# Graph kernel, two layers on one Trainium2 core: half of the middle passes' pick one-hots built on the chip, node rows stored side by side, slot one-hots compared in pairs, overflow tiles shared by sixteen ranges

## The chip, the cores and the metric

The kernel runs on one core of one Trainium2 chip. The metric is the device time of one execution, in microseconds (us). The core has TensorE (PE; its weight loads are shown apart as PEld), VectorE (DVE), ScalarE (ACT), GpSimd (POOL) and SyncE (SP), each with a queue of its own, and 16 DMA engines that all queues share.

## The reference, cut to what matters

There are 32768 nodes with 128 features each and 524288 edges `src -> dst`. Layer 0 sums over edges, adds attention inside blocks of 512 nodes and a feed-forward part; layer 1 runs three passes, each of which sums over the edges in the other direction and adds a lookup in a table of 512 keys.

```python
agg = segment_sum(x[src], dst, num_segments=N)              # layer 0, once
h = relu(((1 + eps) * x + agg) @ W_loc1 + b_loc1) @ W_loc2 + b_loc2
...
for _ in range(3):                                           # layer 1
    retrieved = softmax((x @ Wq.T + bq) @ keys.T) @ values
    agg = zeros_like(x).at[row].add((dinv[:, None] * x)[col])
    lap = x - dinv[:, None] * agg
    x = 0.5 * x + 0.5 * (retrieved - 0.2 * lap)
return layernorm(x1 + layernorm(x))
```

So a sum over edges is needed four times: once in layer 0 (by `dst`) and three times in layer 1 (by `src`).

## The kernel before, in words

**Ranges and slots.** The nodes are cut into 256 ranges of 128. An edge belongs to a pair (own range, other range), and each pair has KS = 6 slots. A value is kept as three bf16 pieces, so a row is ROW = 384 bf16 elements (768 bytes; 772 in layer 0, which also counts edges). To move rows from one range to all others, a *pick* (a one-hot, 128 x 1536, fp8) is multiplied with the rows of a range: `spread` (L1406) makes 12 matmuls of 128x384 per range in six steps `m`, each step into one PSUM tile `exp` of two banks, which ACT casts to bf16 (L1416; every fourth step goes to DVE, in stage 5 every second), and stores two halves of 576 KB per range to `slots` in DRAM (L1419, SP's queue). The next pass fetches, for each range, 1152 KB of slots (`y_i`, L1424, SP's queue).

**What doesn't fit the slots.** Edges beyond six in a pair are listed: five tiles (OW) of 128 indices per range, gathered row by row by GpSimd's indirect DMA (L1429, `listed`), and, where five don't do, SH = 2 more tiles (`common`) that a group of GW = 8 ranges shares and that are gathered once a group. That is 5 + 2/8 = 5.25 gathers a range.

**Adding up.** `hot` (L1438) makes with one DVE instruction (L1440) the one-hots of all NC2 = 19 tiles of a range: 19 x 128 = 2432 elements a partition, comparing a ramp of 1 to 128 with the slot table, one value of which is read 128 times over (a step of 0). `add` (L1444) then makes 19 matmuls of 128x384 into the PSUM tile `seg`, the five listed tiles first. `Sums` (L1455) keeps fetches `lead` ranges ahead (6 in layer 0 and in the last pass, 2 in the middle) with lead + 1 buffers.

**Stages, in order.** (1) Attention, with the sorting of the edges woven in by a quota of DVE time (`edges`, L2120; `build` and `build_more` make the tables). (2) The spread of layer 0 (L1741), which makes its picks on the chip: three matmuls of 128x512 with a column of the identity (`listed_row`, L1385) copy the row of a range to all partitions, and DVE compares each with the partition's number (L1381). (3) The sums of layer 0 (L1802), with its own MLP and the picks of layer 1 (`keep_pick`), which are stored to DRAM, 192 KB a range. (4) The feed-forward part. (5) The first pass of layer 1 (L2035), spread and lookup only. (6) Two middle passes (L2063), in which the sums of block b + 2 are woven with the lookup and the spread of block b; `known_pick` (L1372) loads a pick for each range, two ahead (L1964). (7) The last pass (L2083), sums and two layer norms.

**What sets the order.** In stages 1, 3 and 7 the program's order is kept (`manual_schedule`). In the others the framework orders each engine's instructions by its own plan from the order of emission; in the middle passes the emission is `weave` (L1021) of some 41 steps of lookup and spread over 89 steps of sums per block. PSUM in the middle passes: two `seg` tiles (one bank each), two `exp` tiles (two banks each), one bank for `s`, one for `tr`.

**Rows in DRAM.** Node n = 512 b + 128 c + p lies in row n; a block's tile is [128 partitions p, 4 chunks c, D], so a transfer of a block (`rows_of`, L1316) moves 4 pieces per partition: 768 bytes each for `rows` (L1361), 512 bytes each for `part_d` and `x_d` (L1891, L1958, L1984, L1988).

Of the kernel before, what the change touches and what calls it, by code (L numbers as in the profile page):

```python
# [9 lines left out]
F32 = mybir.dt.float32  # L10
# [9 lines left out]
P = 128  # L20
# [11 lines left out]
OW = 5  # L32
GW = 8
SH = 2
# [375 lines left out]


class Grid:

# [129 lines left out]
    def build(self, pp):  # L543
# [9 lines left out]
        with tc.tile_pool(name="gr", bufs=1) as sp:  # L553
# [13 lines left out]
            for h in range(2):  # L567
                with tc.tile_pool(name=f"gr_h{h}", bufs=1) as hp:
# [89 lines left out]
                    with tc.tile_pool(name=f"gr_c{h}", bufs=1) as ap:  # L658
# [19 lines left out]
                        for t, n in ((0, 3), (3, OW - 3)):  # L678
# [7 lines left out]
                        yield two / 3  # L686
                        nc.vector.tensor_scalar(m, lw, main.oth, P - 1, op0=OP.logical_shift_right,
                                                op1=OP.bitwise_and)
                        yield two / 3
                        nc.vector.tensor_tensor(m, m, key, OP.bitwise_or)  # L690
                        yield one / 3
                        nc.vector.tensor_copy(fb[:, :OL], m)
# [116 lines left out]
    def build_more(self, lane, pp):  # L809
# [12 lines left out]
        with tc.tile_pool(name="mo", bufs=1) as sp:  # L822
# [10 lines left out]
            for h in range(2):  # L833
# [26 lines left out]
                yield L / 1000  # L860
                nc.vector.tensor_scalar(n, word, over.oth, P - 1, op0=OP.logical_shift_right, op1=OP.bitwise_and)
                yield L / 1000
                nc.vector.tensor_tensor(m, m, n, OP.bitwise_or)
                yield L / 1000
                nc.vector.tensor_tensor(val, m, valid, OP.mult)
                yield L / 1000
# [23 lines left out]
def tile_gnn_resnorm(ctx: ExitStack, tc: tile.TileContext, a: dict, out: bass.AP):  # L890
# [417 lines left out]
    def grid_consts(pool):  # L1308
        gc["iota1"] = pool.tile([P, P], BF16, name="iota1")
        nc.vector.tensor_scalar(gc["iota1"], iota, 1.0, None, op0=OP.add)  # L1310
        gc["lane1"] = pool.tile([P, 1], F32, name="lane1")
        nc.vector.tensor_scalar(gc["lane1"], lane_f, 1.0, None, op0=OP.add)
        gc["ident"] = pool.tile([P, P], BF16, name="ident_b")
        nc.vector.tensor_copy(gc["ident"], ident)

    def rows_of(t, i):  # L1316

        return t.rearrange("(b c p) d -> b p c d", c=NCH, p=P)[i]

    def ramp_in_psum(pool):  # L1320

        t = pool.tile([P, P], F32, name="ramp_p")
        nc.vector.tensor_copy(t, gc["iota1"])
        return t

    class Exchange:
# [12 lines left out]
        def load_rows(self, pool):  # L1339
            self.row = pool.tile([P, 2, SL], BF16, name="row")  # L1340
            nc.sync.dma_start(self.row.rearrange("p h f -> p (h f)"), self.grid["row"])

        def load_tables(self, pool):
            self.slot = pool.tile([P, NC2, NW], BF16, name="slot")
            nc.sync.dma_start(self.slot.rearrange("p c w -> p (c w)"), self.grid["slot"])
            self.other = pool.tile([P, NW, OW], I32, name="other")
            nc.scalar.dma_start(self.other.rearrange("p w c -> p (w c)"), self.grid["other"])
            self.shared = pool.tile([P, NW // GW, SH], I32, name="shared")
            nc.scalar.dma_start(self.shared.rearrange("p g c -> p (g c)"), self.grid["shared"])

        def split_steps(self, wp, b, x, rest):


            t = wp.tile([P, NCH, self.width], BF16, name="rows3")
            r = t[:, :, :ROW].rearrange("p c (o d) -> p c o d", o=3)
            if self.width > ROW:
                nc.gpsimd.memset(t[:, :, ROW:], 1.0)

            def end():
                nc.vector.tensor_sub(r[:, :, 2, :], rest, r[:, :, 1, :])  # L1360
                nc.sync.dma_start(rows_of(self.table, b), t)  # L1361
            return t[:, :, :ROW], [lambda: nc.scalar.copy(r[:, :, 0, :], x),
                                   lambda: nc.vector.tensor_sub(rest, x, r[:, :, 0, :]),
                                   lambda: nc.scalar.copy(r[:, :, 1, :], rest), end]
# [73 lines left out]
        def hot(self, wp, i, ramp, bufs):  # L1438
            oh = wp.tile([P, NC2, P], BF16, name="oh", bufs=bufs)
            nc.vector.tensor_tensor(oh, ramp[:, None, :].to_broadcast([P, NC2, P]),  # L1440
                                    self.slot[:, :, i].unsqueeze(2).to_broadcast([P, NC2, P]), OP.is_equal)
            return oh
# [414 lines left out]
    def layer1_grid(v_d, s3, c3):  # L1857

        exs = [Exchange("src", slots_d[t % 2], rows_d[t]) for t in range(T_STEPS)]
        with tc.tile_pool(name="l1g", bufs=1) as gp:  # L1860
# [9 lines left out]
            def first(b, st, wp, p_tr):  # L1870
# [18 lines left out]
                def norm():  # L1889
                    layer_norm(wp, st["x0"], st["x"])  # L1890
                    nc.sync.dma_start(rows_of(xs_d[0], b), st["x"])  # L1891
                return load, [(7, scale), (12, turn), (15, norm)]
# [26 lines left out]

            def emit(t, b, st, wp, p_e, p_s, p_tr, share):  # L1920

                ex = exs[t]
                y = {}

# [26 lines left out]
                def remain():  # L1951
# [5 lines left out]
                    nc.vector.scalar_tensor_tensor(part, st["x"], 0.4, part, op0=OP.mult, op1=OP.add)  # L1957
                    nc.sync.dma_start(rows_of(part_d, b), part)  # L1958
# [21 lines left out]
            def ask_part(t, b, wp):  # L1980

                if b < NB:
                    p_i = wp.tile([P, NCH, D], F32, name="part_i", bufs=3)
                    nc.scalar.dma_start(p_i, rows_of(part_d, b))  # L1984
                    parts[b] = [p_i]
                    if t == T_STEPS - 1:
                        x1 = wp.tile([P, NCH, D], F32, name="x1", bufs=3)
                        nc.scalar.dma_start(x1, rows_of(xs_d[0], b))  # L1988
                        parts[b].append(x1)
# [68 lines left out]
            with tc.tile_pool(name="l1w", bufs=2) as wp, \  # L2058
                    tc.tile_pool(name="l1_seg", bufs=2, space=PSUM) as p_g, \
                    tc.tile_pool(name="l1_exp", bufs=2, space=PSUM) as p_e, \  # L2060
                    tc.tile_pool(name="l1_s", bufs=1, space=PSUM) as p_s, \
                    tc.tile_pool(name="l1_tr", bufs=1, space=PSUM) as p_tr:
                for t in range(T_STEPS - 1):  # L2063
# [3 lines left out]
                    for w0 in range(2):  # L2067
                        ask_pick(wp, w0)
                    for n in range(-2, NB):
# [3 lines left out]
                        if n >= 0:  # L2073
                            lists.append(emit(t + 1, n, sts[n], wp, p_e, p_s, p_tr, 4))
                        two_b = placed(*lists)
# [102 lines left out]
```

## Time and profile before

| what | value |
|---|---|
| median of 3 runs (lowest, highest) | 14195.87 us (14195.01, 14202.4) |
| the profiled execution's own time | 14201.3 us |
| its span in the profile | 14199.4 us |
| mean granted TensorE clock | 0.927 |
| PE, DVE, ACT, POOL busy, share of the span | 86%, 80%, 47%, 43% |

| stage | from, to (us from the span's start) |
|---|---|
| 1 attention and sorting | 0 to 3530 |
| 2 spread of layer 0 | 3530 to 4531 |
| 3 sums of layer 0 | 4540 to 6232 |
| 4 feed-forward | 6250 to 6490 |
| 5 first pass of layer 1 | 6490 to 7965 |
| 6 two middle passes | 7965 to 12471 |
| 7 last pass | 12471 to 14199 |

The stages' bounds are the first and last start of their own instructions in the trace. A group's line gives the line of the kernel, the engine, the operation, what is written and read, how often, the busy time and the mean of one. DMA shares are the summed time of the packets over 16 engines; they can come out above 1. A line of waits names the waiting engine and line, who released it, the time in all, how often, and the longest.

### The profile page before, as it was taken

How to read it: one execution, taken by the hardware profiler on the slowest of the kernel's cores; microseconds unless marked ns; L12 is line 12 of the kernel's file. 1: busy time of each engine (PE TensorE's matmuls, PEld its weight loads, DVE VectorE, ACT ScalarE, POOL GpSimd, SP SyncE). 2: the span in 40 equal slices, each digit the busy share in tenths (PEclk: the TensorE clock that was granted, in tenths of full speed). 3: DMA queues.
4: the chain of work that ended last, by engine and by line, in shares of the span. 5: the costliest groups of instructions: out<-in, count | busy, mean ns of one | idle time of the engine just before them, and what ended most of it. 6: DMA issues, size and time to landing. Idle time of an engine off the chain costs nothing. (4 is left out here: it accounts for less than half of the span.)

```text
span 14199.4 us, 168166 instructions
## 1 busy us (share of the span) xinstructions
PE 12173.8 (86%) x58982; PEld 5828.9 (41%) x58982; DVE 11413.1 (80%) x16677; ACT 6658.1 (47%) x10316; POOL 6079.5 (43%) x5461
## 2 busy tenths in 40 slices
PE   8888888889887888888998799999899999966666
PEld 3232223333333444444444355555455555533333
DVE  7998998776998888877888677777677777778888
ACT  4343444334987111127888566666566666610000
POOL 0000000000001777740000477877688878767777
PEclk9898888888999999999999999999999999987787
DMA  1000000000999999977888899999999999988887
GB/s 40 11 11 17 10 11 12 18 8 33 348 346 348 309 309 309 310 242 261 304 311 308 299 383 385 390 383 383 350 376 386 382 391 381 383 292 285 286 283 256
DMA packets 1640075, 3602.99 MB, mean 254 GB/s; under 512 B 199346, under 2 KB 976466, under 8 KB 1638066
## 3 DMA queue, kind: packets, MB, share of 16 engines
q1 hardware_dynamic: 1165424, 2936.81, 55.6%
q0 software_dynamic: 258752, 533.02, 12.3%
q10 hardware_dynamic: 215042, 122.32, 2.8%
q8 instruction: 465, 7.62, 0.2%
q14 instruction: 392, 3.21, 0.1%
HBM read 2088.45 MB, written 1503.00 MB: 253 GB/s over the span
## 5 line engine op out<-in xcount | busy, mean ns | idle before, releaser
L1429 POOL DMA_INDIRECT listed<-rows,other x5120 | 5725.6, 1118 | 3544.2 <-issue 3151.1
L1416 ACT CAST y_o<-exp 128x768 bf16<-128x768 f32 x4224 | 3224.0, 808 | 1271.9 <-DMA slots<-y_o 627.2
L1411 PE MATMUL exp<-rows,pick 128*128 128x384 bf16 x12288 | 2768.2, 326 | 394.9 <-ACT y_o L1416 289.4
L1453 PEld LDWEIGHTS <-oh 128*128 128x128 bf16 x19456 | 1992.2, 102 | 2648.8 <-issue 1629.8
L1453 PE MATMUL seg<-y_i,oh 128*128 128x384 bf16 x12288 | 2745.0, 349 | 9.3 <-DMA y_i<-slots 9.3
L1416 DVE CAST y_o<-exp 128x768 bf16<-128x768 f32 x1920 | 1830.9, 954 | 687.4 <-PE exp L1411 636.2
L1411 PEld LDWEIGHTS <-pick 128*128 128x128 fp8e4 x12288 | 1185.1, 97 | 2115.5 <-issue 1550.7
L1453 PE MATMUL seg<-listed,oh 128*128 128x384 bf16 (+1 forms) x5120 | 1257.6, 336 | 815.5 <-DMA listed<-rows,other 777.2
L1606 ACT ACTIVATE pT<-s 128x1024 f32<-128x1024 f32 x1024 | 1021.5, 1023 | 1353.7 <-PE s L1602 1351.3
L1586 DVE TENSOR_REDUCE mx<-s 128x2 f32<-128x1024 f32 x1024 | 1204.4, 1219 | 270.5 <-PE s L1580 270.2
L1440 DVE TENSOR_TENSOR oh<-ramp_p,slot 128x2432 bf16<-128x2432 f32 x512 | 1372.3, 2681 | 12.7 <-DMA slot<-slot_dst 9.4
L1440 DVE TENSOR_TENSOR oh<-iota,slot 128x2432 bf16<-128x2432 bf16 x512 | 1373.7, 2683 | 3.0 <-DMA slots<-y_o 3.0
L283 POOL DMA_INDIRECT c_r<-pivots_over,c_ix x2 | 1.9, 946 | 3056.7 <-DVE c_ix L281 3056.4
L1602 PE MATMUL s<-ql,k 32*128 32x512 f32 x4096 | 1032.4, 692 | 259.2 <-DVE mx L1586 244.6
L2005 DVE SCALAR_TENSOR_TENSOR part_i<-seg,dinv,part_i 128x128 f32<-128x128 f32 x1536 | 529.6, 345 | 543.0 <-PE seg L1453 531.9
L1064 ACT ACTIVATE ln_rs<-ln_mv,eps_c 128x4 f32<-128x4 f32 x192 | 57.1, 297 | 1670.8 <-DVE ln_mv L1062 1489.7
L1930 PE MATMUL s<-keysT,qT 128*128 128x512 f32 x1536 | 818.2, 615 | 7.3 <-ACT pr L1043 3.7
L1453 PE MATMUL seg<-common,oh 128*128 128x384 bf16 (+1 forms) x2048 | 600.7, 350 | 194.5 <-DMA common<-rows,shared 194.2
L1942 PE MATMUL s<-pt,values 128*128 128x512 f32 x1536 | 750.6, 600 | 10.8 <-ACT pt L1937 10.6
L1580 PE MATMUL s<-k,q 32*128 32x512 f32 x4096 | 745.2, 726 | 6.0 <-DVE mx L1586 2.6
L1613 PE MATMUL pv<-pT,vx 128*32 128x512 f32 x4096 | 698.6, 751 | 0.2 <-ACT pT L1606 0.2
L1388 PE MATMUL row_p<-row,ident_b 128*128 128x512 bf16 x1536 | 601.8, 392 | 82.9 <-DVE pick L1381 62.3
(393 smaller groups left out, 14180.8 us busy)
## 6 DMA issues: line engine op xcount, KB each, us to landing
slots<-y_o SPq DMA_DIRECT2D x2048, 576.0 KB
y_i<-slots SPq DMA_DIRECT2D x1024, 1152.0 KB
pick<-pick SPq DMA_DIRECT2D x1024, 192.0 KB
listed<-rows,other POOLq DMA_INDIRECT x5120
rows<-rows SPq DMA_DIRECT2D x192, 384.0 KB
part_d<-part_o SPq DMA_DIRECT2D x192, 256.0 KB
part_i<-part_d ACTq DMA_DIRECT2D x192, 256.0 KB
rows<-rows SPq DMA_DIRECT2D x64, 386.0 KB
```

What stands on the lines that cost most here:

```text
L1411: nc.tensor.matmul(ps[:, j, :ROW], pick[:, o:o + P], r, start=True, stop=True)
L1416: (nc.vector.tensor_copy if to_dve else nc.scalar.copy)(dst, ps[:, :, :ROW])
L1429: nc.gpsimd.indirect_dma_start(out=g[:, k, :], out_offset=None, in_=self.table, in_offset=bass.IndirectOffsetOnAxis(ap=index[:, k:k + 1], ...
L1440: nc.vector.tensor_tensor(oh, ramp[:, None, :].to_broadcast([P, NC2, P]), self.slot[:, :, i].unsqueeze(2).to_broadcast([P, NC2, P]), OP.is ...
L1453: nc.tensor.matmul(ps[:, :n], oh[:, j, :], src, start=(k == 0), stop=(k == NC2 - 1))
L1580: nc.tensor.matmul(two[s // 2][:, s % 2, :], t["q", o][32 * s:32 * s + 32, c * P:(c + 1) * P], t["k", o][32 * s:32 * s + 32, :], start=Tru ...
L1586: nc.vector.tensor_reduce(m[:, c, 2 * i:2 * i + 2, xr[o]], st[b]["two"][i], AX.X, OP.max, negate=True)
L1602: nc.tensor.matmul(two[s // 2][:, s % 2, :], t["k", o][32 * s:32 * s + 32, c * P:(c + 1) * P], t["ql", o][32 * s:32 * s + 32, :], start=Tr ...
L1606: nc.scalar.activation(t["p", c][:, 2 * i:2 * i + 2, :], two[i], AF.Exp)
L1613: nc.tensor.matmul(t["o"][32 * s:32 * s + 32, :], t["v"][:, c, s, 2 * o:2 * o + 2, :].rearrange("p z e -> p (z e)"), t["p", c][:, s, :], s ...
L1930: nc.tensor.matmul(s, st["q"][:, c * P:(c + 1) * P], keysT, start=True, stop=True)
L1942: nc.tensor.matmul(ps, values[:, k, :], st["pt"][:, k, :], start=(k == 0), stop=(k == NCH - 1))
```

## The change

Four edits come together.

1. `GW` goes from 8 to 16: the two `common` tiles are shared by sixteen ranges, so 5.125 gathers a range.
2. Rows side by side: `kept_of` lays node (b, c, p) at row 512 b + 4 p + c, so that a block's transfer is one piece per partition (3072 bytes for `rows`, 2048 for `part_d` and `x_d`). The indices of the gathers have to name these rows: `row_index` makes them in `build` and `build_more`. The kernel's input and output stay as they were.
3. Pairs: the slot table is kept twice side by side, range first, so that the last dimension of every operand of `hot` is two bf16 elements next to each other; the two copies are made by DVE when the table is loaded (once in layer 0, once in layer 1). The ramp in PSUM (layer 0, last pass) becomes bf16, by a transpose on PE. In the middle passes the ramp is `iota1` in SBUF, as before.
4. In the middle passes every odd range's pick is made on the chip (`pick_steps`), during the spread of the even range before it: three matmuls of 128x512 into two `exp` tiles, ahead of the spread's steps 1 and 3, and two DVE comparisons of 1024 and 512 elements. Only the even ranges' picks are loaded. `row` (768 KB) is loaded once, ahead of the passes. In the first pass of layer 1 all picks are still loaded.

```diff
-GW = 8
+GW = 16
...
+def row_index(nc, dst, spare, window, lane):
+    n = NCH.bit_length() - 1
+    cost = dst.shape[-1] / 1000
+    lane(dst)
+    yield cost
+    nc.vector.tensor_scalar(dst, dst, n, None, op0=OP.logical_shift_left)
+    yield cost
+    nc.vector.tensor_scalar(spare, window, 7, NCH - 1, op0=OP.logical_shift_right, op1=OP.bitwise_and)
+    yield cost
+    nc.vector.tensor_tensor(dst, dst, spare, OP.bitwise_or)
+    yield cost
+    nc.vector.tensor_scalar(spare, window, 7 + n, 7 + n, op0=OP.logical_shift_right, op1=OP.logical_shift_left)
+    yield cost
+    nc.vector.tensor_tensor(dst, dst, spare, OP.bitwise_or)
+    yield cost
...
+        gc["down"] = pool.tile([P, P], BF16, name="down")
+        nc.vector.tensor_copy(gc["down"], gc["lane1"].to_broadcast([P, P]))
...
+    def kept_of(t, i):
+        return t.rearrange("(b p c) d -> b p (c d)", c=NCH, p=P)[i]
...
     def ramp_in_psum(pool):
-        t = pool.tile([P, P], F32, name="ramp_p")
-        nc.vector.tensor_copy(t, gc["iota1"])
+        t = pool.tile([P, P], BF16, name="ramp_p")
+        nc.tensor.transpose(t, gc["down"], gc["ident"])
         return t
...
         def load_tables(self, pool):
-            self.slot = pool.tile([P, NC2, NW], BF16, name="slot")
-            nc.sync.dma_start(self.slot.rearrange("p c w -> p (c w)"), self.grid["slot"])
+            self.slot = pool.tile([P, NW, NC2, 2], BF16, name="slot")
+            with tc.tile_pool(name="slot_l", bufs=1) as lp:
+                t = lp.tile([P, NC2, NW], BF16, name="slot_1")
+                nc.sync.dma_start(t.rearrange("p c w -> p (c w)"), self.grid["slot"])
+                for o in range(2):
+                    nc.vector.tensor_copy(self.slot[:, :, :, o], t.rearrange("p c w -> p w c"))
...
-                nc.sync.dma_start(rows_of(self.table, b), t)
+                nc.sync.dma_start(kept_of(self.table, b), flat(t))
...
+        def pick_steps(self, wp, pp, tag, w, keep):
+            def part(j, n):
+                if j == 0:
+                    keep[w] = wp.tile([P, SL], FP8, name="pick", bufs=3)
+                ps = pp.tile([P, 2, BLK], F32, name="exp", tag=tag)
+                for k in range(n):
+                    nc.tensor.matmul(ps[:, k, :], gc["ident"][:, w % P:w % P + 1].to_broadcast([P, P]),
+                                     self.row[:, w // P, (j + k) * BLK:(j + k + 1) * BLK], start=True, stop=True)
+                nc.vector.tensor_scalar(keep[w][:, j * BLK:(j + n) * BLK], ps[:, :n].rearrange("p k n -> p (k n)"),
+                                        gc["lane1"], None, op0=OP.is_equal, saturate=False)
+            return [lambda: part(0, 2), lambda: part(2, 1)]
...
         def hot(self, wp, i, ramp, bufs):
             oh = wp.tile([P, NC2, P], BF16, name="oh", bufs=bufs)
-            nc.vector.tensor_tensor(oh, ramp[:, None, :].to_broadcast([P, NC2, P]),
-                                    self.slot[:, :, i].unsqueeze(2).to_broadcast([P, NC2, P]), OP.is_equal)
+            nc.vector.tensor_tensor(oh.rearrange("p c (w z) -> p c w z", z=2),
+                                    ramp.rearrange("p (w z) -> p w z", z=2)[:, None].to_broadcast([P, NC2, P // 2, 2]),
+                                    self.slot[:, i].unsqueeze(2).to_broadcast([P, NC2, P // 2, 2]), OP.is_equal)
...
-                    if m == 0:
+                    if m == 0 and not (made and i % 2):
                         ask_pick(wp, i + 2)
+                    if made and m == 0 and i % 2 == 0:
+                        making[:] = exs[0].pick_steps(wp, p_e, "exp", i + 1, picked)
+                    if making and m in (1, 3):
+                        making.pop(0)()
```

Left out are the calls that `kept_of` replaces for `part_d` and `x_d` (stored at L1891 and L1958, loaded at L1984 and L1988), the two places where `row_index` replaces an index of two instructions (L687 to L690, L861 to L863), and the flag `made`, which only the middle passes set.

More of the change, by code (lines that the diff above doesn't have):

```diff
@@ L686, in build @@
                         yield two / 3
[L687 to L691, printed above, removed]
+                        yield from row_index(
+                            nc, m, fb[:, :OL].bitcast(I32), key,
+                            lambda t: nc.vector.tensor_scalar(t, lw, main.oth, P - 1, op0=OP.logical_shift_right,
+                                                              op1=OP.bitwise_and))
                         nc.vector.tensor_copy(fb[:, :OL], m)
@@ L860, in build_more @@
                 yield L / 1000
[L861 to L865, printed above, removed]
+                yield from row_index(
+                    nc, n, val.bitcast(I32), m,
+                    lambda t: nc.vector.tensor_scalar(t, word, over.oth, P - 1, op0=OP.logical_shift_right,
+                                                      op1=OP.bitwise_and))
+                nc.vector.tensor_tensor(val, n, valid, OP.mult)
                 yield L / 1000
@@ L1318, in rows_of, with flat @@
         return t.rearrange("(b c p) d -> b p c d", c=NCH, p=P)[i]
+    def kept_of(t, i):
+        return t.rearrange("(b p c) d -> b p (c d)", c=NCH, p=P)[i]
+    def flat(t):
+        return t.rearrange("p c d -> p (c d)")
     def ramp_in_psum(pool):
-        t = pool.tile([P, P], F32, name="ramp_p")
-        nc.vector.tensor_copy(t, gc["iota1"])
+        t = pool.tile([P, P], BF16, name="ramp_p")
+        nc.tensor.transpose(t, gc["down"], gc["ident"])
         return t
@@ L1339, in load_rows @@
         def load_rows(self, pool):
-            self.row = pool.tile([P, 2, SL], BF16, name="row")
+            self.row = pool.tile([P, 2, SL], BF16, name="row", bufs=1)
             nc.sync.dma_start(self.row.rearrange("p h f -> p (h f)"), self.grid["row"])
         def load_tables(self, pool):
-            self.slot = pool.tile([P, NC2, NW], BF16, name="slot")
-            nc.sync.dma_start(self.slot.rearrange("p c w -> p (c w)"), self.grid["slot"])
+            self.slot = pool.tile([P, NW, NC2, 2], BF16, name="slot")
[4 more added lines that the diff above has]
+                    nc.vector.tensor_copy(self.slot[:, :, :, o], t.rearrange("p c w -> p w c"))
             self.other = pool.tile([P, NW, OW], I32, name="other")
@@ L1890, in norm @@
                     layer_norm(wp, st["x0"], st["x"])
-                    nc.sync.dma_start(rows_of(xs_d[0], b), st["x"])
+                    nc.sync.dma_start(kept_of(xs_d[0], b), flat(st["x"]))
                 return load, [(7, scale), (12, turn), (15, norm)]
@@ L1918, in prepare, with emit @@
                         (14, lambda: st["split"][3]())]
-            def emit(t, b, st, wp, p_e, p_s, p_tr, share):
+            def emit(t, b, st, wp, p_e, p_s, p_tr, share, made=False):
                 ex = exs[t]
-                y = {}
+                y, making = {}, []
                 def scores(c):
@@ L1957, in remain @@
                     nc.vector.scalar_tensor_tensor(part, st["x"], 0.4, part, op0=OP.mult, op1=OP.add)
-                    nc.sync.dma_start(rows_of(part_d, b), part)
+                    nc.sync.dma_start(kept_of(part_d, b), flat(part))
                 def spread(n):
@@ L1983, in ask_part @@
                     p_i = wp.tile([P, NCH, D], F32, name="part_i", bufs=3)
-                    nc.scalar.dma_start(p_i, rows_of(part_d, b))
+                    nc.scalar.dma_start(flat(p_i), kept_of(part_d, b))
                     parts[b] = [p_i]
@@ L1987, in ask_part @@
                         x1 = wp.tile([P, NCH, D], F32, name="x1", bufs=3)
-                        nc.scalar.dma_start(x1, rows_of(xs_d[0], b))
+                        nc.scalar.dma_start(flat(x1), kept_of(xs_d[0], b))
                         parts[b].append(x1)
@@ L2062, in layer1_grid @@
                     tc.tile_pool(name="l1_tr", bufs=1, space=PSUM) as p_tr:
+                exs[0].load_rows(wp)
                 for t in range(T_STEPS - 1):
@@ L2066, in layer1_grid @@
                     ask_part(t, 0, wp)
-                    for w0 in range(2):
-                        ask_pick(wp, w0)
+                    ask_pick(wp, 0)
                     for n in range(-2, NB):
@@ L2073, in layer1_grid @@
                         if n >= 0:
-                            lists.append(emit(t + 1, n, sts[n], wp, p_e, p_s, p_tr, 4))
+                            lists.append(emit(t + 1, n, sts[n], wp, p_e, p_s, p_tr, 4, True))
                         two_b = placed(*lists)
```

## The prediction, on record before the result

> **What bounds the kernel now.** I cut the span into stages with the table of busy time by windows (us, then busy us and instructions of PE, PEld, DVE, ACT, POOL, the clock, the DMA share, GB/s).
>
> ```profile
> 3550.00:4500.00 950.00, 802.23 (x3684) 352.63 (x3684) 892.84 (x1230) 857.77 (x1227) 6.57 (x62) 1.00 0.92 347
> 4600.00:6200.00 1600.00, 1310.19 (x6327) 701.70 (x6326) 1422.09 (x2553) 177.64 (x426) 1208.40 (x1279) 0.93 0.94 309
> 6500.00:7700.00 1200.00, 1086.45 (x4996) 578.01 (x4997) 1042.72 (x2000) 1062.75 (x1765) 0.00 (x0) 0.99 0.85 303
> 8600.00:9800.00 1200.00, 1134.77 (x5786) 622.19 (x5785) 879.38 (x1152) 733.61 (x1219) 954.53 (x733) 1.00 1.02 384
> ...
> 12700.00:14100.00 1400.00, 901.51 (x4002) 448.57 (x4001) 1143.41 (x2365) 31.20 (x105) 1063.58 (x1105) 0.80 0.86 285
> ```
>
> Spread of layer 0: DVE works 94%. First pass of layer 1: PE, ACT and DVE each 87 to 91%. The middle (4506 us of 14199, the fourth row) has PE at 95% and DMA at 1.02. The two stages of pure sums (second and fifth row) show POOL at only 76%, which misleads; the last pass's gathers tell why:
>
> ```profile
> L1429 POOL DMA_INDIRECT listed<-rows,other x1053: 942/946/1457, 12699.1 to 14099.4; - x176
> ...
>   PE seg L1453: 387.9, 255
> ```
>
> A gather takes 0.946 us, and after each, POOL sits 0.30 us on "issue" (247.1 us in 811 waits of the window 12800 to 14000). Start to start is 1400/1105 = 1.267 us here and 1600/1279 = 1.251 us in layer 0: POOL never stops, and PE waited 388 us for what it fetches. Both stages end with POOL.
>
> In the middle, waits and the timeline:
>
> ```profile
> ACT y_o L1416 <- DMA slots<-y_o: 182.5, 80, 5.6
> POOL listed L1429 <- issue: 176.1, 578, 0.3
> ...
> PE exp L1411 <- ACT y_o L1416: 54.4, 95, 2.8
> ...
> POOL listed L1429 <- PE seg L1453: 29.4, 37, 4.7
> ```
>
> ```profile
> 9004.28 0.95 POOL L1429 DMA_INDIRECT listed<-rows,other  x1 [0.30 <-issue]
> ...
> 9005.42 2.68 DVE L1440 TENSOR_TENSOR oh<-iota,slot 128x2432 bf16<-128x2432 bf16 x1
> 9005.53 3.40 POOL L1429 DMA_INDIRECT listed<-rows,other  x1 [0.30 <-issue]
> ...
> 9009.23 0.95 POOL L1429 DMA_INDIRECT listed<-rows,other  x1 [0.30 <-issue]
> ```
>
> PE's longest wait is for ACT to clear `exp`, ACT's is for stores of `y_o` to land. And a gather that meets `hot` lasts until 0.8 us after `hot` ends. Three resources are tight. A range takes 1200 us x 5.25/733 = **8.6 us**. POOL: 5.25 x 1.25 = 6.57, plus 1.73 of prolonging (954.53 busy less 733 x 0.947, over 139.6 ranges) = 8.3. DMA: 1.02 x 8.6 = 8.75. PE: by start-to-start steps of the timeline, a bf16 matmul 0.163 us (31 a range), an fp32 one of 512 columns 0.43 (18 a block), a transpose 0.108 (24 a block): 5.05 + 2.6 = 7.65 of work, 8.13 with switching (busy 95%).
>
> **What the Trainium skill says.** "SBUF — State Buffer", section "Who interferes with whom": a VectorE instruction with two SBUF inputs contends with a GpSimd instruction that reads SBUF, one with at most one SBUF input doesn't. The trace agrees: `hot` with its ramp in SBUF stretches gathers, with the ramp in PSUM (layer 0, last pass) the longest gather lasts 0.96 and 1.46 us. "Vector Engine (DVE) Microarchitecture Reference", section "5.1 Performance modes — why throughput varies by op and dtype": an innermost row of two 2-byte elements at step 1 runs at two elements a cycle, PSUM source or not; one element re-read at step 0 ran at one. The second half agrees: 2432 elements in 2.68 us is 0.91 a ns. Nothing in the trace shows the first. Price, from "VectorE: DVE Perf Modes", "Side-by-side: where the cycles go for N=2048 bf16" (some 150 cycles + N/2 at 0.96 GHz): estimate (150 + 1216)/0.96 = 1.42 us.
>
> **The change part by part.**
>
> *GW 16*: 32 gathers fewer a pass. Layer 0's sums: 32 x 1.251 = **-40 us**; last pass: 32 x 1.267 = **-41 us**. Is the next limit far enough? The range falls from 6.57 to 6.41 us and from 6.65 to 6.49. Layer 0's DVE (89%) drops with `hot`; its DMA goes from 0.94 to some 0.96, less than the middle carries. I count all of it. In the middle a gather's bytes cost 0.28 us of all engines (DMA queue view of 8600 to 9800: 17.1% x 1200/733); an eighth of that is 0.035 us a range.
>
> *Pairs*: `hot` 2.68 to 1.42 us, if the mode takes hold; 2.68 otherwise, both kept. DVE time is no limit in the stages of sums, so nothing there. In the middle DVE loses 1.26 us a range, and a gather that meets `hot` is held some 0.7 us instead of 1.8: POOL falls to 5.125 x 1.25 + 0.7 = **7.1 us**, no longer a limit. Loading: two copies of 4864 strided elements, bounded by two and one elements a cycle, 2.7 to 5.2 us each. Layer 0: POOL's first gather starts at 4542.7, 2 us after the table lands, so I take **+4 us** (0 to +10, if the copies hold POOL). Layer 1: DVE's queue starts the first pass behind them, **+5 us** (0 to +10). The ramp by transpose: under 1 us.
>
> *Rows side by side*: a 512-byte piece costs 27 ns of one engine (queue 10: 2.6% of 16 x 1200 us over 18480), a 2048-byte one 95 (feed-forward: 64.3% of 16 x 110 us over 13276, less semaphores), so four for one saves at least 13 ns. A block in the middle has three such transfers of 128 partitions: 3 x 128 x 13/16 = 0.31 us, 0.08 a range (0.14 if a large piece alone costs less than under load). Stages 2 and 5 have other bounds: nothing. The indices: `row_index` adds three shifts and one OR per half, 3 x 0.555 + 0.958 (rows L684, L690) and 3 x 0.62 + 1.09 (L861, L863), twice each: 11 us of DVE. `build`'s lies where DVE works over 90%, `build_more`'s where it works 67% beside PE: **+7 us** (0 to +11).
>
> *Picks on the chip*: removed, 192 KB for each second range. A 1536-byte piece lies between the two prices, 72 ns: 128 x 72/16 = 0.58 us, 0.29 a range. With rows and gathers, DMA falls by 0.40 to **8.35 us**. Added on PE: three matmuls of 128x512. "TensorE: Matmul & The Clock Gate", "Back-to-back issue gap", gives N/2.4 + 2.5 ns, which fits the 163 ns at 384; so 0.216 us each, 0.32 a range: PE **7.97 to 8.45 us**. Added on DVE: 512 elements cost 0.744 (L1381), 1024 then 0.744 + 512/0.96 = 1.28: 1.01 a range, less than `hot` gives back (6.3 us becomes 6.05). Added on `exp`: seven tiles a range in the place of six, on two buffers, and these two are cleared by DVE, whose queue may have `hot` in front. Behind that wait stands all of PE's queue. This is the unknown: 0 if the planner finds sums to put in between, up to 1.45 us an odd range (rival D). SP's queue loses half its pick loads and gains none; `row` is 768 KB once, 2 us.
>
> So the middle: POOL 7.1, DMA 8.35, PE 7.97 to 8.45, where it was 8.3, 8.75, 7.65 to 8.13. DMA and PE now meet. I take **8.45 us** a range: PE's upper end; the present waits on stores shrink with DMA's load and make room for those on the comparisons. 512 ranges x (8.6 - 8.45) = **-77 us**.
>
> Sum against the profiled 14201.3: -40 - 41 - 77 + 4 + 5 + 7 = -142: 14059, **14060**. The median shown lies 5 us below the profiled run, which changes nothing.
>
> **The rivals.**
> *B, PE has air*: its work is the 7.97, and the middle follows DMA, with large packets at their cheapest: 8.2 us. 512 x 0.4 = -205 in place of -77: 13931. For: PE's only long wait today goes back to DMA. Against: PE is busy 95%.
> *C, PE takes back the gain of the middle* (8.6 us stays): 14136. For: PE at 95% and 0.32 more.
> *E, the pairs don't double `hot`*: POOL stays at 8.2, DVE at 7.3: the middle some 8.7 (+51): 14187.
> *D, slower: `exp` blocks PE.* The two-bank part holds its buffer for its matmuls, then 1.28 us of DVE plus some 0.2 of hand-over. PE needs that buffer again after one spread (0.33) and about 3.7 sums (0.60), so it stands 0.55 us with DVE free, and some 0.4 more behind other DVE work: 0.9 us an odd range, 0.45 a range on 8.45 = 8.9. 512 x 0.3 = +154: 14290. With the one-bank part waiting as well (0.5), it would be 14420. It decides once the middle loses 65 us, the gain elsewhere: 8.73 us, a stall of some 0.55 us an odd range.
>
> **How the numbers follow.** A 0.46, B 0.22, C 0.10, E 0.07, D 0.15. A measurement of this kernel can tell about 0.2% (28 us) from no change. A, B and C are faster (0.78), E is the same (0.07), D slower (0.15). Range: B's time less the loading costs gives 13900 below; above I take D's milder half, 14250.
>
> **What would show it.** Right: `hot` near 1.42 us; gathers that meet it near 1.7 us in the middle; 1312 gathers a pass at 1.25 and 1.27 us; DMA share under 1 and a range of 8.3 to 8.6 us in the middle. Wrong: PE waiting for DVE's `pick` on `exp` for over 0.5 us an odd range (D), `hot` at 2.68 (E), POOL with idle time in the last pass (the 81 us not earned), or a longer attention stage.

## The result and the profile after

The changed kernel takes 14148.27 us (median of 8 runs, 14140.83 to 14161.45), the kernel before 14200.35 us beside it: a ratio of 0.9961, 95% interval 0.995 to 0.9972. By the ratio that is 55 us less, where 142 were forecast (the two medians differ by 52). The profiled execution takes 14156.93 us, its span is 14155.1 us.

Busy time by windows of the kernel after, with the columns of before (us, busy us and instructions of PE, PEld, DVE, ACT, POOL, the clock, the DMA share, GB/s): sums of layer 0, the middle, the last pass.

```profile
4600.00:6150.00 1550.00, 1280.53 (x6305) 685.82 (x6304) 1140.67 (x2546) 176.61 (x423) 1171.69 (x1240) 0.96 0.94 315
8600.00:9800.00 1200.00, 1142.21 (x5944) 648.34 (x5942) 831.49 (x1282) 749.11 (x1214) 717.27 (x710) 0.99 1.00 368
...
12700.00:14050.00 1350.00, 881.03 (x3927) 438.46 (x3927) 866.25 (x2325) 30.91 (x104) 1026.08 (x1064) 0.80 0.85 289
```

In the stages of sums a gather still starts every 1550/1240 = 1.250 and 1350/1064 = 1.269 us, so GpSimd still ends them, with fewer gathers. In the middle GpSimd's busy time fell from 954.53 to 717.27 us, and what the transfers moved from 384 to 368 GB/s. Both were meant to happen, and yet a range takes 8.65 to 8.70 us from compare to compare, where it took 8.56 to 8.59.

Groups of instructions in the middle (count, busy us, mean ns; then idle time before them and what ended it):

```profile
L1474 POOL DMA_INDIRECT listed<-rows,other x692 | 700.7, 1013 | 480.9 <-PE seg L1499 287.0 <-issue 172.7 <-DMA listed<-rows,other 17.6
...
L1485 DVE TENSOR_TENSOR oh<-iota,slot 128x2432 bf16<-128x2432 bf16 x138 | 195.2, 1414 | 0.0
...
L1433 DVE TENSOR_SCALAR pick<-exp,lane 128x1024 fp8e4<-128x1024 f32 (+1 forms) x138 | 139.5, 1011 | 41.2 <-PE exp L1431 41.2
```

The compare takes 1.414 us, and a gather 1013 ns on average where the 733 of before took 1302. GpSimd now waits 287 us for TensorE: it is ahead of it. In layer 0 and the last pass, with its ramp in PSUM, the compare takes as long (duration in ns, least, median, longest):

```profile
L1485 DVE TENSOR_TENSOR oh<-ramp_p,slot x512: 1405/1414/1426, 4545.4 to 14123.2; 128x2432 bf16<-128x2432 bf16 x171
```

The waits in the same window (us in total, times, longest us):

```profile
POOL listed L1474 <- PE seg L1499: 287.0, 100, 9.7
ACT y_o L1461 <- PE exp L1456: 270.9, 338, 2.8
...
ACT y_o L1461 <- DMA slots<-y_o: 62.0, 35, 5.6
...
PEld s L1959 <- ACT pr L1061: 43.7, 35, 5.4
...
PE s L1959 <- ACT pr L1061: 30.5, 26, 5.0
PE exp L1431 <- ACT y_o L1461: 23.7, 19, 2.4
```

ScalarE's wait for the stores of `y_o` fell from 182.5 to 62.0 us, and its wait for TensorE's spread rose from 58.6 to 270.9: ScalarE too stands behind TensorE. TensorE itself has one wait that it did not have, for a tile of `exp` at the pick's row matmuls (L1431), and one that has grown: at the query (L1959), for a buffer that ScalarE's softmax reads. The same wait before:

```profile
PE s L1913 <- ACT pr L1043: 6.3, 32, 0.2
```

Its wait at the spread, 54.4 us before, is down to 0.8. One wait of the new kind in the timeline (start, duration, idle time before):

```profile
9019.46 0.80 ACT L1461 CAST y_o<-exp 128x768 bf16<-128x768 f32 x1 [2.52 <-DMA slots<-y_o]
...
9020.31 0.59 PE L1431 MATMUL exp<-row,ident_b 128*128 128x512 bf16 x2 [1.22 <-ACT y_o L1461]
...
9020.94 1.28 DVE L1433 TENSOR_SCALAR pick<-exp,lane 128x1024 fp8e4<-128x1024 f32 x1 [0.43 <-PE exp L1431]
```

The stages, by the starts of their first instructions in the two traces (us):

| stage | before | after | difference | forecast |
|---|---|---|---|---|
| attention, to its last normalisation | 3525.8 | 3531.9 | +6 | +7 |
| sums of layer 0, first to last gather | 1681 | 1643 | -38 | -40, and +4 for loading |
| start of layer 1, from the end of the feed-forward to the first turn | 22.4 | 35.2 | +13 | +5 |
| the middle, from its first compare to the last pass' first | 4507.6 | 4529.5 | **+22** | **-77** |
| last pass | 1724 | 1686 | -38 | -41 |

The stages between these are 9 us shorter together. What is missing lies in the middle (99 us) and at the start of layer 1 (8 us). The 6 us of the attention stage are less than its spread: it ends between 3511 and 3532 us in the kernels here that have `row_index`, and between 3510 and 3533 us in those that haven't.

### The profile page after: what moved, and what is told of

It reads as the page before. It is cut to its first block, busy times and chain, and to the rows that moved or that the text cites. A ratio compares the mean times of both kernels' runs of the same rounds, so it can differ in the third digit from the quotient of the medians.

```text
span 14155.1 us, 170063 instructions
## 1 busy us (share of the span) xinstructions
PE 12190.3 (86%) x59752; PEld 5910.8 (42%) x59752; DVE 10680.1 (75%) x17208; ACT 6721.6 (47%) x10316; POOL 5185.7 (37%) x5333
## 5 line engine op out<-in xcount | busy, mean ns | idle before, releaser
L1474 POOL DMA_INDIRECT listed<-rows,other x5120 | 5042.8, 985 | 4431.2 <-issue 3153.5
L1461 ACT CAST y_o<-exp 128x768 bf16<-128x768 f32 x4224 | 3282.5, 805 | 1667.4 <-PE exp L1456 1191.1
L1456 PE MATMUL exp<-rows,pick 128*128 128x384 bf16 x12288 | 2809.4, 325 | 214.3 <-ACT y_o L1461 113.7
L1499 PE MATMUL seg<-listed,oh 128*128 128x384 bf16 (+1 forms) x5120 | 1334.0, 335 | 860.5 <-DMA listed<-rows,other 847.4
L1444 DVE TENSOR_SCALAR_CACHE_REDUCE pick<-row_p,lane 128x512 fp8e4<-128x512 f32 x768 | 555.6, 746 | 248.3 <-PE row_p L1420 235.7
L1485 DVE TENSOR_TENSOR oh<-iota,slot 128x2432 bf16<-128x2432 bf16 x512 | 724.3, 1415 | 3.0 <-DMA slots<-y_o 3.0
L1485 DVE TENSOR_TENSOR oh<-ramp_p,slot 128x2432 bf16<-128x2432 bf16 x512 | 723.5, 1414 | 3.4 <-DMA slots<-y_o 3.3
```

The costliest lines, as they stand in the source:

```text
L1456: nc.tensor.matmul(ps[:, j, :ROW], pick[:, o:o + P], r, start=True, stop=True)
L1461: (nc.vector.tensor_copy if to_dve else nc.scalar.copy)(dst, ps[:, :, :ROW])
L1474: nc.gpsimd.indirect_dma_start(out=g[:, k, :], out_offset=None, in_=self.table, in_offset=bass.IndirectOffsetOnAxis(ap=index[:, k:k + 1], ...
L1485: nc.vector.tensor_tensor(oh.rearrange("p c (w z) -> p c w z", z=2), ramp.rearrange("p (w z) -> p w z", z=2)[:, None].to_broadcast([P, NC2 ...
L1499: nc.tensor.matmul(ps[:, :n], oh[:, j, :], src, start=(k == 0), stop=(k == NC2 - 1))
```

## The experiments

**Theory 1**: in the middle TensorE became the bound, and the row matmuls of the made one-hots ate what the other parts gave. **Theory 2**: the transfers still bound it. **Theory 3**: the two `exp` tiles are held up, by VectorE's compare or by the extra turn. The first four kernels ran on one chip; the kernel before took 14195.88 us there.

**All one-hots loaded.** The changed kernel without its last part:

```diff
-                            lists.append(emit(t + 1, n, sts[n], wp, p_e, p_s, p_tr, 4, True))
+                            lists.append(emit(t + 1, n, sts[n], wp, p_e, p_s, p_tr, 4))
-                    ask_pick(wp, 0)
+                    for w0 in range(2):
+                        ask_pick(wp, w0)
```

> The changed kernel with one part undone: the one-hot of the slots of every middle range is loaded again, none is made on the chip; pairs, rows side by side and sixteen ranges a tile stay. Theory 1 (TensorE is the bound of the middle now, and the three 128x512 row matmuls of every odd range, 0.66 us or +0.33 us a range, ate what the shorter compare gave): the middle goes from 4529 us, first compare to the last pass' first, down by 100 to 150 us, to about 4390 to 4430, and the kernel to about 14000 to 14050. Theory 2 (the transfers are still the bound; the picks relieved them and something else cost time): the middle grows by up to 0.29 us a range, to about 4600 to 4680, and the kernel takes about 14220 to 14300. Theory 3 (the tiles of exp are held up, not TensorE's time): like theory 1, 4390 to 4430; the next two kernels tell 1 from 3.

Measured: 13948.39 us, 0.9826 (0.9812 to 0.9839); the middle takes 4327.5 us, 8.26 a range. The middle fell further than any of the theories expected. Windows and waits of this kernel's middle:

```profile
8600.00:9800.00 1200.00, 1166.89 (x6012) 653.48 (x6011) 737.73 (x1196) 766.47 (x1272) 789.72 (x745) 1.00 1.03 398
```

```profile
PE exp L1456 <- ACT y_o L1461: 21.6, 49, 1.2
...
PE seg L1499 <- DMA y_i<-slots: 4.4, 7, 2.1
```

TensorE is busy 97.2% and waits little. The transfers, with every one-hot loaded and the same large pieces, carry 398 GB/s, so the 368 of the changed kernel were no ceiling. Making every second one-hot on the chip costs 0.9961 - 0.9826 = 1.35% of 14200, **192 us**. For the changed kernel theory 2 is out.

**The row matmuls alone.** One-hots loaded; the odd ranges' row matmuls run too, into `exp` tiles that nothing reads (extra work; the compare is left out):

```diff
-                    if m == 0 and not (made and i % 2):
+                    if m == 0:
                         ask_pick(wp, i + 2)
...
-                nc.vector.tensor_scalar(keep[w][:, j * BLK:(j + n) * BLK], ps[:, :n].rearrange("p k n -> p (k n)"),
-                                        gc["lane1"], None, op0=OP.is_equal, saturate=False)
```

> As the kernel with all one-hots loaded, but the row matmuls of the odd ranges run too, into tiles of exp that nothing reads (extra work; nothing of the result depends on it). Against it, theory 1 (TensorE's time) expects the whole cost here: +0.33 us a range, some +130 to +170 us in 512 ranges, since the transfers are not relieved. Theory 2 (transfers) expects nothing, within 20 us. Theory 3 (exp held by VectorE's compare of the pick) expects little here, under 40 us, because no VectorE step stands between these tiles and their release.

Measured: 14141.97 us, 0.9964 (0.995 to 0.9978); the middle 4528.8 us. The whole cost is there, 196 us over the loaded kernel in 0.9964 - 0.9826, without any VectorE step; theory 1 had expected 130 to 170.

**Row matmuls and compares**, the compare into a tile `pick_x` that nothing reads:

```diff
-                    keep[w] = wp.tile([P, SL], FP8, name="pick", bufs=3)
+                    keep[w] = wp.tile([P, SL], FP8, name="pick_x", bufs=2)
```

> As the one before with the VectorE compares of the odd ranges as well, into a tile that nothing reads: everything that making a one-hot costs, without the transfer that it saves. Theory 1 expects it within 40 us of the one before. Theory 3 expects the cost to come here: 60 to 150 us over the one before. The changed kernel itself is this one less the transfer of half of the one-hots: theory 1 expects the changed kernel 0 to 60 us faster than this one, theory 2 over 100 us faster.

Measured: 14155.33 us, 0.9969 (0.9959 to 0.9979). The compares add nothing that can be told apart, so theory 3's first form is out. Against this kernel the changed one only saves the transfer of half the one-hots, and TensorE's order is the same in both traces (61 of 62 blocks of the first middle pass): 0.9961 against 0.9969, intervals overlapping. **The saved transfer is worth nothing measurable** once TensorE does the row matmuls.

**Every one-hot made**, none but the first loaded:

```diff
-                    if m == 0 and not (made and i % 2):
+                    if m == 0 and not made:
                         ask_pick(wp, i + 2)
-                    if made and m == 0 and i % 2 == 0:
+                    if made and m == 0 and i + 1 < NW:
```

> The changed kernel with the one-hot of every middle range made on the chip, none but the first loaded: twice the row matmuls and compares, no transfer of one-hots. Theory 1 (TensorE) expects +0.25 to +0.33 us a range, 130 to 170 us more than the changed kernel: about 14270 to 14320. Theory 2 (transfers) expects it faster than the changed kernel by 0.1 to 0.25 us a range: about 14020 to 14100. Theory 3 (exp held) expects over 170 us more, about 14320 to 14450, with the waits at the pick matmuls more than doubled.

Measured: 14256.24 us, 1.0047 (1.0033 to 1.0062), the middle 4633.2 us. Slower than the kernel before, as theory 1 had the direction, but 122 us over the changed kernel by the ratios, and 104 by the middle, where it expected 130 to 170. TensorE's idle time fell from 58 to 46 us of 1200 beside it, and its wait at the query is gone from the list:

```profile
8600.00:9800.00 1200.00, 1154.13 (x5931) 650.31 (x5998) 923.71 (x1381) 733.72 (x1182) 693.70 (x692) 0.99 0.97 349
```

**Time or turn?** The kernel with the row matmuls alone, cut to 8 columns each: the `exp` tiles turn just as often, TensorE works a fraction.

```diff
-                    nc.tensor.matmul(ps[:, k, :], gc["ident"][:, w % P:w % P + 1].to_broadcast([P, P]),
-                                     self.row[:, w // P, (j + k) * BLK:(j + k + 1) * BLK], start=True, stop=True)
+                    nc.tensor.matmul(ps[:, k, :8], gc["ident"][:, w % P:w % P + 1].to_broadcast([P, P]),
+                                     self.row[:, w // P, (j + k) * BLK:(j + k) * BLK + 8], start=True, stop=True)
```

Beside it, on the same chip (before: 14202.03 us), the full row matmuls again, and the kernel before with only `GW = 16` and the pairs, which is the loaded kernel without the rows side by side.

> The loaded kernel with the row matmuls of the odd ranges 8 columns wide, beside the one with full row matmuls on the same chip. TensorE's time as the cost of a made one-hot: over 0.8% faster than the full ones on any chip (on one where the kernel before takes about 14200: 0.983 to 0.988 of it). The turn of the exp tiles, or the number of instructions, as the cost: within 0.3% of the full ones.

> The loaded kernel with the full row matmuls of the odd ranges, which nothing reads: 0.996 of the kernel before where that takes about 14200, as before. Here it is what the 8-column ones are compared with.

> The kernel before with sixteen ranges a tile and pairs: the loaded kernel without the rows side by side. Where the kernel before takes about 14200: 0.982 to 0.983 if the larger packets of the rows are worth nothing there, 0.984 to 0.986 if 0.04 to 0.1 us a range, over 0.99 if they make most of the loaded kernel's gain. Where it takes 15000 or more: 0.999 to 1.001, as on two such chips.

| kernel | us | ratio, interval | middle, us |
|---|---|---|---|
| 8-column row matmuls | 13967.77 | 0.9837 (0.9823 to 0.985) | 4347.0 |
| full row matmuls | 14160.33 | 0.9972 (0.9959 to 0.9984) | 4538.6 |
| `GW` and pairs alone | 14126.08 | 0.9946 (0.9932 to 0.9959) | 4510.9 |

The 8-column form costs about 16 us over the loaded kernel (0.9837 against 0.9826, within the intervals), the full one 192 more. One more turn of the tiles alone isn't the cost on this chip, so theory 3's second form is out too. The same window of the 8-column and of the full kernel:

```profile
8600.00:9800.00 1200.00, 1166.24 (x6200) 654.10 (x6199) 736.00 (x1189) 760.73 (x1262) 798.62 (x740) 1.00 1.03 396
```

```profile
8600.00:9800.00 1200.00, 1141.11 (x5958) 652.59 (x5957) 698.54 (x1142) 749.42 (x1212) 737.39 (x713) 0.99 1.02 381
```

The full form gets through 713 gathers where the 8-column form gets through 740, with TensorE busy 95% and not 97%: its own waits come on top. The wait at the query stands again in its list of waits:

```profile
PE s L1955 <- ACT pr L1061: 33.2, 27, 2.9
...
PE exp L1429 <- ACT y_o L1457: 21.9, 22, 1.7
```

**What this does not part.** The framework plans each kernel anew, and in the traces of these two no block of the first middle pass (0 of 62) has TensorE's other instructions in the same order. The kernels with and without compares differ in this way too. The wait at the query may belong to the order: 33.2 us here, none in the list of the 8-column kernel. So wide row matmuls are shown to cost 192 us where narrow ones cost 16; how much of that is their own time and how much the other order was not measured apart. An estimate from their start-to-start time in the changed kernel, 0.216 us: 3 x 0.216 x 256 = 166 us are their own.

**Compare or packets?** The third kernel gives the surprise. `GW` and pairs leave the middle where it was (4510.9 against 4507.6 us), though the compare takes its short time and the gathers that meet one are prolonged by 0.50 us a range in place of 1.79. TensorE's order is another here than in the kernel before; what pairs do in the old order was not run. The rows side by side, which are all that the loaded kernel has over this one, are worth 0.9946 - 0.9826 = 1.2%, **170 us**, and here TensorE's order is the same in both traces (62 of 62 blocks of the first middle pass). The two ran on different chips, but on the chip of this one the 8-column kernel, which has the rows and some work more, is 1.1% faster than it, and the full row matmuls gave nearly the same middle on both chips (4528.8 and 4538.6 us). Waits and DMA queues of the middle of this kernel (queues: packets, MB, share of 16 engines), then the queues of the loaded kernel:

```profile
PE seg L1460 <- DMA y_i<-slots: 32.0, 37, 3.1
...
PEld L1417 <- DMA pick<-pick: 18.6, 27, 1.1
...
PE exp L1417 <- DMA pick<-pick: 7.9, 19, 0.7
```

```profile
DMA packets 185148, 453.79 MB, mean 378 GB/s; under 512 B 21665, under 2 KB 103285, under 8 KB 185068
...
q1 hardware_dynamic: 133324, 374.76, 81.3%
...
q10 hardware_dynamic: 18078, 8.98, 2.5%
```

```profile
DMA packets 153527, 477.91 MB, mean 398 GB/s; under 512 B 22942, under 2 KB 53392, under 8 KB 153441
...
q1 hardware_dynamic: 112526, 394.21, 83.1%
...
q10 hardware_dynamic: 5238, 9.52, 2.1%
```

With the small pieces TensorE waits for slots and one-hots to land; with the large ones 4.4 us are left of the first, and the second is gone. Per range the packets go from 1336 to 1056, and their summed time over 16 engines from 8.77 to 8.47 us, worked out from the records of both windows: 0.14 of it is the pieces' own time (medians of 27 ns for 512 bytes and 84 for 2048, 36 for 768 and 121 for 3072), the rest is that the 4608-byte packets take 186 ns on average in place of 191, with the same median of 178. That the small pieces slowed these is not shown: beside large pieces they take 194 ns in the full kernel and 198 in the changed one. So without large pieces transfers did hold TensorE in the middle. Of the 0.36 us a range that they win, the pieces' own time explains 0.14; how the rest comes about stays open.

**Other chips.** Eleven runs came to three chips on which the kernel before takes 15019, 15155 and 15009 us. In the sums of layer 0 (4600 to 6150) 103 to 111 of some 1055 gathers there start over 2 us after the one before, some 15 us apart, where elsewhere at most two of 1240 do. Other waits rule there, so these are read only among themselves. Each row is a kernel: the kernel before with one part alone (`GW = 16`; the pairs; the rows with their indices), with `GW` and pairs, the 8-column kernel, and the loaded kernel with layer 1's slot pairs made by GpSimd in the first pass:

```diff
-            exs[0].load_tables(gp)
+            exs[0].load_tables(gp, later=True)
...
+                    if n == 0:
+                        exs[0].pair_slots(wp, nc.gpsimd.tensor_copy)
```

> The kernel before with the common part gathered for sixteen ranges in the place of eight, and nothing else. By the prediction's account the sums of layer 0 lose 32 gathers, 40 us, and the last pass 41 us: 14120. The middle: unchanged if TensorE and the lengthened gathers bound it, 20 to 60 us less if every gather there counts: 14060 to 14100. If the first compare's 2.68 us becomes the limit of layer 0's sums (VectorE is at 89% there), under 30 us come there.

> The kernel before with the compare on pairs (a two-byte ramp, the slot table doubled by two copies a layer) and nothing else. The loaded kernel won 180 us in the middle without made one-hots. If that is the shorter compare, which no longer lengthens the gathers, the middle falls from 4508 to about 4330 to 4380 here, the copies cost 4 us in layer 0 and 13 us in layer 1, and the sums stay as they were: 14050 to 14090. If it is the larger packets of the rows, the middle falls by under 50 us and the kernel takes 14160 to 14210.

> The kernel before with the rows of a block side by side in memory and the indices worked out to match, and nothing else. By the prediction's account 0.08 us a range in the middle if the transfers bound it (40 us), and 7 us for the indices: 14165. If the transfers do not bound the middle, nothing comes back and the indices cost 7 us: 14195 to 14210. If the larger packets are what the loaded kernel won in the middle: 14020 to 14060.

> As the kernel whose odd ranges run the row matmuls into tiles of exp that nothing reads, with each matmul 8 columns wide in the place of 512 (nothing reads these either): the tiles of exp turn just as before, one more in seven, but TensorE's work for it falls from 0.65 us to under 0.2 us an odd range. If the cost of a made one-hot is TensorE's time, most of the 194 us between the loaded kernel (13948) and that one (14142) goes: 13960 to 14020. If it is the turn of the exp tiles (a spread has to wait for one more release), most stays: 14090 to 14150.

> The kernel before with the compare on pairs alone, once more, for the same reason. If the shorter compare won the middle (gathers no longer lengthened): 0.989 to 0.993 of the kernel before, with the middle near 4330 to 4380 us where the kernel before has 4508. If on its first chip it was slower (1.005) for a reason of its own, a wait that the pairs bring, it is slower here too, and the wait is to be seen at the first compare or at the stores: 1.00 to 1.005.

> The kernel with the 8-column row matmuls once more, since its first run came to a chip on which the kernel before takes 15019 us. The expectation stands, as a ratio to the kernel before on the same chip: the loaded kernel has 0.983, the one with full row matmuls 0.996. TensorE's time as the cost: 0.983 to 0.988. The turn of the exp tiles as the cost: 0.992 to 0.996.

> The kernel before with sixteen ranges a tile and pairs, so the loaded kernel without the rows side by side. If the larger packets of the rows are worth nothing in the middle, it has the loaded kernel's 0.983, or 6 us less since the indices stay cheap. If the transfers bound the middle by their packets, 0.04 to 0.1 us a range come on top: 20 to 50 us, 0.984 to 0.986. If rows side by side make most of what the loaded kernel won: over 0.99.

> The loaded kernel with layer 1's slot pairs made by GpSimd in the first pass, where it has nothing to do, in the place of VectorE ahead of it. If the 13 us at the start of layer 1 were the two copies and their wait, 10 to 13 us come back: 0.9815 to 0.982 of the kernel before. If GpSimd's copies hold VectorE in the first pass, or the start of layer 1 waits for something else, 0 to 5 us: 0.9825 to 0.983.

> The loaded kernel with the row matmuls of the odd ranges 8 columns wide, into tiles of exp that nothing reads, again: both earlier runs came to chips on which the kernel before takes 15019 and 15155 us. On a chip where it takes about 14200: TensorE's time as the cost of a made one-hot: 0.983 to 0.988 of the kernel before. The turn of the exp tiles as the cost: 0.992 to 0.996.

> The kernel before with sixteen ranges a tile and pairs, again on another chip. Where the kernel before takes about 14200: the larger packets of the rows worth nothing: 0.982 to 0.983. Worth 0.04 to 0.1 us a range in the middle: 0.984 to 0.986. Making most of the loaded kernel's gain: over 0.99.

> The loaded kernel with layer 1's slot pairs made by GpSimd during the first pass, again on another chip. Where the kernel before takes about 14200: 10 to 13 us less than the loaded kernel, 0.9815 to 0.982, if the copies and their wait were the 13 us; 0.9825 to 0.983 if not.

| kernel | 15019 us | 15155 us | 15009 us |
|---|---|---|---|
| `GW = 16` alone | 0.9922 (0.9909 to 0.9935) | | |
| pairs alone | 1.0047 (1.0033 to 1.0061) | 1.0093 (1.0079 to 1.0108) | |
| rows alone | 0.9998 (0.9989 to 1.0006) | | |
| `GW` and pairs | | 1.0006 (0.9999 to 1.0013) | 0.9994 (0.9985 to 1.0002) |
| loaded, copies on GpSimd | | 0.9984 (0.9977 to 0.9991) | 0.9951 (0.9935 to 0.9968) |
| 8-column row matmuls | 1.029 (1.0274 to 1.0305) | 1.0017 (1.001 to 1.0023) | 1.0279 (1.0262 to 1.0296) |

There the pairs alone cost 0.5 to 0.9%, and the 8-column kernel is up to 2.9% slower than before. Beside the loaded kernel with copies on GpSimd it is 3.3% slower on the chip of 15009 us (1.0279 against 0.9951) and 0.3% on that of 15155. Neither is explained, and so the little that the 8-column form costs is shown for chips like the first alone. What the rows or the pairs alone do on a chip like the first was not run. One thing can be read from the last kernel all the same, in stages that last as long on all these chips: with the copies on GpSimd (8.8 us each) the first turn of layer 1 comes 14 us sooner after the feed-forward, but the first compare of the middle then follows it by 1480 and 1482 us, where it takes 1466 to 1469 without. **Nothing is won**: the start of layer 1 gives its 13 us to the first pass.

## Why the prediction was wrong, point by point

*Sums of layer 0 and last pass, -40 and -41*: right, -38 each. GpSimd never stopped, so gathers left out came back at their start-to-start time.

*Pairs*: the compare's 1.42 us was right (1.414), from SBUF and from PSUM, at the two elements a cycle that the Trainium skill, "Vector Engine (DVE) Microarchitecture Reference", section "5.1 Performance modes — why throughput varies by op and dtype", gives for such rows. POOL's fall in the middle was right in direction. Before, 139 of 140 compares prolonged a gather by over 0.5 us, 1.79 us a range in all; with `GW` and pairs alone it is 0.50 and in the loaded kernel 0.57, near the 0.7 that was taken. In the changed kernel it is 0.25, but there no gather runs during 43 of the 138 compares, since GpSimd waits for TensorE. A compare with two SBUF inputs still holds a gather that it meets, as the Trainium skill, "SBUF — State Buffer", section "Who interferes with whom", has it. The sum that led to 8.3 has a slip: 954.53 less 733 x 0.947, over 139.6, is 1.87 and not 1.73. But POOL's load was not shown to be a limit: with it gone, `GW` and pairs moved the middle by 3 us.

*Rows, 0.08 us a range*: the mechanism right, the size wrong. The loaded kernel's middle is 183 us shorter than with `GW` and pairs alone, 0.36 us a range; the pieces' own saving was 0.14, the step's upper figure, and what makes up the rest is open.

*Loading and indices*: the +7 for `row_index` can be neither borne out nor refuted, since the end of the attention stage spreads by over 20 us; that +6 was measured is luck. Layer 0's +4 did not come: the first gather starts at 4541.7 us, 1 us sooner than before. Layer 1's +5 measured +13: each copy took 5.6 us, above the upper bound of 5.2, and they waited for the table.

*The middle, 8.45 us a range, -77 us*: **this is the step that failed**. It reads: "I take 8.45 us a range: PE's upper end; the present waits on stores shrink with DMA's load and make room for those on the comparisons". TensorE's work was sized well: start to start it is 7.56 us a range before and 7.92 after, where 7.65 and 7.97 were taken. What failed is the waiting beside it. The prediction let it shrink to 0.48 us of switching; measured, it fell from 1.01 to 0.76 us a range, less than the 0.36 that the work grew. Of the 0.76, the waits at the query and at the pick are 0.22 and 0.17 (30.5 and 23.7 us over 138 ranges). The loaded kernel shows how little room there was: at 97.2% busy it has 7.58 of work and 0.67 beside it, and a range of 8.26. So three row matmuls of 0.216 us for each second range, 0.32 a range or 166 us, came on top, and waits with them: 192 to 202 us in all. Whether another order of the same instructions would be free of these waits stays open. The waits on stores did shrink, but they were ScalarE's.

Against that stood -0.29 us a range of transfer, which the prediction also counted (0.27 by the packets' records). It is worth nothing once TensorE is late. Nor was the packets' summed time the floor that the prediction's 8.75 and 8.35 were taken for: the loaded kernel runs a range in 8.26 us with 8.47. The sum of the middle by part, across chips: `GW` and pairs +3, rows -183, picks +202: +22.

*Rivals*: C, "PE takes back the gain of the middle", with 14136 us, comes nearest, at a chance of 0.10, and by its mechanism too. That its number fits is in part luck: the middle lost 22 us where C has it unchanged, out of a gain of 183 us by a part that was given 41 and a loss of 202 where the row matmuls' own time makes 166. D's mechanism, `exp` blocked until VectorE has compared, did not show: the compares add nothing, and the wait at the pick is for ScalarE. B, TensorE with air, is refuted by the row matmuls alone, which cost 196 us with no transfer saved. E is refuted by the 1.414 us.

The version to keep, on chips like the first, is the loaded kernel, the change less its last part: 13948.39 us, 1.7% under the kernel before, and 1.4% under the changed one (0.9826/0.9961 = 0.986). On the slow chips only its form with copies on GpSimd was run, and won 0.2 to 0.5%.

## What to carry to other kernels

Where two resources of a stage are both near their limit, moving work from one to the other is no gain in itself: here 0.27 us a range of transfer saved were worth nothing, and 0.32 of TensorE's time cost 0.38 to 0.39. Beside an engine's work count all the waiting that its traces show, and not the switching alone: even at 97% busy this one had 0.67 us a range beside 7.58 of work. Where a planner orders the instructions, compare the order in the traces before a difference is put down to one part. And ask of each part of a bundled change what it does alone: one part won 170 us, another lost 192, and the whole showed 55.

## What the runs showed of the hardware that was not expected

- A piece four times as large took the DMA engines 16 to 22% less per byte: 84 ns for 2048 bytes against 4 x 27 for 512, and 121 for 3072 against 4 x 36 for 768. Block rows in the large pieces took the middle from 378 to 398 GB/s, more than this alone explains.
- The packets' summed time is no lower bound: the loaded kernel takes 8.26 us a range (a DMA share of 1.03), though its packets sum to 8.47 us over 16 engines.
- A gather that meets a compare with both inputs in SBUF ended 0.81 to 0.83 us after the compare, whether that took 2.68 us (before) or 1.41 (after).
- Chips differ: the same kernel takes 14196 to 14202 us on some and 15009 to 15155 on three others, with the attention stage alike and pauses between gathers, and parts of this change have another sign there.
- Copying 4864 two-byte elements with a large step in the source took 5.6 us on VectorE, less than one element a ns, and 8.8 us on GpSimd.
